# Twenty-eight pairs of unread products on TensorE ahead of the first transposes of a graph-network stack

## The chip, the core and the metric

The kernel runs on one core of a Trainium2 chip. The core's engines are TensorE (PE in the profile; its weight loads are PEld), VectorE (DVE), ScalarE (ACT), GpSimd (POOL) and SyncE (SP), which here issues the loads from HBM. The metric is the time of one execution on the device in microseconds (us), lower is better.

## The reference

A stack of four graph layers over N = 3327 nodes with D = 64 features and a dense 3327 x 3327 matrix `adj` of weights, most of them zero. Every layer normalizes, clips at zero, propagates and adds to x:

```python
# layer 0: two GRU cells, each with one propagation
def _ggc(x, adj, W, wih, whh, bih, bhh):
    m = adj @ (x @ W)
    gi = m @ wih.T + bih
    gh = x @ whh.T + bhh
    ...
    return (1.0 - z) * n + z * x
h = jnp.maximum(_layernorm(x, axis=-1), 0.0)
x = x + _L0_gnn_ref(h, adj, ...)
# layer 1: weights 0.5 ** (rank from the end of the row's neighbours), one propagation
# layer 2: w = adj * adj, three times x = w @ x; x = x @ W.T + b
# layer 3: twice x = tanh(concat([adj @ x, x]) @ W[k])
```

In all there are eight propagations, each a product of a 3327 x 3327 matrix with a 3327 x 64 one.

## The kernel before

The nodes are padded to 3328 = 26 blocks of 128. The host hands over `adj` transposed; x lies in SBUF as `xs`, 128 partitions by 13 blocks by two halves by 64 features. It is loaded in two transfers (line 119): first the blocks of chunk 0 (three blocks, 384 columns of 128 partitions), then the rest.

The 13 blocks are cut into four chunks of 3, 3, 3 and 4 blocks, in two groups (chunks 0 and 1; chunks 2 and 3). A tile of the adjacency is 128 source nodes by the columns of one group in both halves, 768 or 896 KB; SyncE loads the tiles (line 405) in the order of their use into 20 slots, each load waiting until its slot is free.

A propagation (`propagate`, line 607) takes one tile and one chunk and issues two f32 matmuls, one for each half, with 64 output partitions and 384 or 512 columns each; both halves share a PSUM bank and use the upper and lower 64 partitions. The list `units` holds all these steps in the order in which TensorE runs them. It begins with `alone(0, 0, ...)`: the first propagation for group 0, one tile after the other, chunk 0 then chunk 1. Beside it a count of nonzero entries runs (`count`, line 542, bf16 matmuls on a mask which VectorE makes at line 466).

Everything on an engine runs in the order in which the program issues it. Ahead of the list come four tasks `before_0`, one for each chunk, which the program advances in a fixed interleaving:

```python
def before_0(c):
    h = nodes(c)
    yield from layernorm_relu(h, c)
    y[0][c] = h
    yield 12.0 + 3.0 * c
    transpose_to_features(h, c)
```

`layernorm_relu` (lines 834 to 849) is VectorE work except for one power on GpSimd (line 845); it writes the features `y`. `transpose_to_features` (line 791) turns chunk c's features by six f32 matmuls with the identity on TensorE, and ScalarE copies the result out (line 793). The transposes of chunk 0 are the first instructions on TensorE, and the propagation follows.

PSUM has eight banks, four named `sum` and four named `temp`. `take()` hands out a free one, `give(i)` returns it; which one is next follows from how long ago each was returned. Nothing else schedules: bank choices and order are made when the program is built.

Of the kernel before, what the change touches and what calls it, by code (L numbers as in the profile page):

```python
# [91 lines left out]
def upper(n):  # L92
    return slice(n * D, (n + 1) * D)
# [3 lines left out]
def kernel(  # L97
# [9 lines left out]
    nc = tc.nc  # L107
# [9 lines left out]
    xs = const.tile([P, NB, 2, D], F32, name="xs")  # L117
# [39 lines left out]
    def unfold_cell(cell):  # L157

        n = 3 * D + (NBIAS if cell == 0 else 0)
        i, ps = take()  # L160
        for h in range(2):
            nc.tensor.matmul(ps[upper(h), :n], ident[:, :D], stage[:, 4 * D:4 * D + n], start=True, stop=True)
        v = ps[:, :3 * D].rearrange("p (g f) -> p g f", f=D)
        for h in range(2):
            nc.vector.tensor_copy(cells[upper(1 - h), cell, h, 0:3], v[upper(1 - h)])
        if cell == 0:
            nc.vector.tensor_copy(bcol, ps[:, 3 * D:n])
        give(i)

    def fold_cell(cell):  # L170
# [67 lines left out]
    def more_constants():  # L238
# [7 lines left out]
        load_cell(0)  # L246
        yield 20.0
        unfold_cell(0)
        yield 1.0

# [27 lines left out]
        load_cell(1)  # L278
        yield 20.0
        unfold_cell(1)  # L280
        yield from fold_cell(1)
        yield 30.0
# [13 lines left out]
    def blocks(c):  # L296
        return CH[c][1] - CH[c][0]

    def width(c):
        return blocks(c) * P  # L300
# [15 lines left out]
    def take(sums=False, either=True):  # L316


        either = either and not sums
        pool = idle_sums if sums else idle_temps  # L320
        if either and idle_sums and (not pool or released[idle_sums[0]] < released[pool[0]]):
            pool = idle_sums
        for c in list(tasks):
            if not pool and c not in running:
                advance(c)
        i = pool.popleft()
        return i, banks[i]

    def give(i):
        released[i] = max(released) + 1  # L330
        (idle_sums if i < 4 else idle_temps).append(i)
# [5 lines left out]
    def flat(t):  # L337
        return t.rearrange("p b s d -> p b (s d)")
# [4 lines left out]
    def xchunk(c):  # L343
        return xs[:, CH[c][0]:CH[c][1]]
# [8 lines left out]
    def advance(c):  # L353
        running.add(c)
        try:
            tasks[c][1] = next(tasks[c][0])
        except StopIteration:
            del tasks[c]
        running.discard(c)

    def begin(c, task):
        finish(c)
        tasks[c] = [task, 0.0]
        advance(c)
# [274 lines left out]
    def alone(g, k, sweep, lag=None, parts=False):  # L639
        tiles = [Tile(q, g, KIND[k] == SQUARED) for q in sources_of(*range(NC))]  # L640
        counting = Counting(g, lag)
        chunks = (GROUPS[g][0], *PARTS) if parts else GROUPS[g]
        for t in tiles[:NQ - sweep]:
            for c in chunks:
                put(k, c, t)
            if lag is not None:
                counting.add(t)
        for c in chunks:
            for t in tiles[NQ - sweep:]:
                put(k, c, t)  # L650
                if lag is not None and c == GROUPS[g][0]:
                    counting.add(t)
        counting.rest()
# [277 lines left out]
# [6 lines that stand above are left out]
# [96 lines left out]
    joint(1, 6, sweep=8, later=4, keep=4)  # L1033
    alone(0, 7, sweep=6, parts=True)

    for c in (0, 0, 1, 0, 1, 2, 1, 2, 3, 2, 3, 3):
        if c in tasks:
            advance(c)
        else:
            begin(c, before_0(c))  # L1040
# [45 lines left out]
```

## Time and profile before

| | |
|---|---|
| time, median of 3 runs | 706.93 us (705.94 to 707.05) |
| span of the profiled execution, first to last instruction | 703.7 us |
| other time of the profiled execution | none is given on its page |
| TensorE busy | 679.8 us, 97% of the span |
| VectorE, ScalarE, GpSimd busy | 350.1, 271.8, 80.0 us |
| first matmul | at 14.92 us |
| mean granted TensorE clock | 0.999 |
| read from HBM | 199.45 MB, 285 GB/s over the span |

The runs' times are of whole executions on the device; the profile's span runs from the first to the last instruction of one execution, and its times are counted from the span's start. A row such as `128*64 128x384 f32` is a matmul with 128 rows in, 64 out and 384 columns. `x12` is a number of records. Text in brackets is the idle time of the engine before the row and what ended it.

### The profile page before, as it was taken

How to read it: one execution, taken by the hardware profiler on the slowest of the kernel's cores; microseconds unless marked ns; L12 is line 12 of the kernel's file. 1: busy time of each engine (PE TensorE's matmuls, PEld its weight loads, DVE VectorE, ACT ScalarE, POOL GpSimd, SP SyncE). 2: the span in 40 equal slices, each digit the busy share in tenths (PEclk: the TensorE clock that was granted, in tenths of full speed). 3: DMA queues.
4: the chain of work that ended last, by engine and by line, in shares of the span. 5: the costliest groups of instructions: out<-in, count | busy, mean ns of one | idle time of the engine just before them, and what ended most of it. 6: DMA issues, size and time to landing. Idle time of an engine off the chain costs nothing.

```text
span 703.7 us, 12628 instructions
## 1 busy us (share of the span) xinstructions
PE 679.8 (97%) x5100; PEld 372.9 (53%) x5100; DVE 350.1 (50%) x746; ACT 271.8 (39%) x422; POOL 80.0 (11%) x114
## 2 busy tenths in 40 slices
PE   1999999999999999999999999999999999999997
PEld 1454666643556787677444444333344444344586
DVE  7556835643997889847523105425271565005101
ACT  1014100122146888888998206832166600000101
POOL 4300000002284233111100000000000000000000
PEclk9999999999999999999999999999999999999999
DMA  9999996089686952683799649973998399927991
GB/s 344 401 385 404 406 405 241 2 314 398 209 279 253 371 177 76 246 297 96 265 390 343 245 151 409 405 276 100 398 366 271 107 391 406 406 81 276 402 403 45
DMA packets 68549, 201.31 MB, mean 286 GB/s; under 512 B 7228, under 2 KB 8228, under 8 KB 68492
## 3 DMA queue, kind: packets, MB, share of 16 engines
q1 hardware_dynamic: 65596, 199.46, 75.9%
q8 instruction: 40, 0.66, 0.4%
q10 hardware_dynamic: 720, 0.85, 0.3%
q0 software_dynamic: 2176, 0.20, 0.2%
q14 instruction: 17, 0.14, 0.1%
HBM read 199.45 MB, written 0.85 MB: 285 GB/s over the span
## 4 chain that ended last, share of the span: by engine, by line
PE 91%; DVE 7%; issue 0%; ACT 0%; DMA 0%; POOL 0%; ACTq 0%; DVEq 0%; POOLq 0%
PE sum L607 77%; PE temp L307 5%; PE temp L542 2%; PE temp L876 2%; PE sum L307 1%; DVE adj L466 1%; PE temp L774 1%; PE sum L876 1%; DVE e L521 1%; DVE st L842 1%; DVE adj L901 1%; DVE t L836 1%; DVE y L841 0%; DVE st L834 0%; DMA xs<-in_x 0%
## 5 line engine op out<-in xcount | busy, mean ns | idle before, releaser
L607 PE MATMUL sum<-adj,y 128*64 128x384 f32 (+3 forms) x3016 | 534.5, 502 | 0.7 <-DVE y L849 0.6
L607 PEld LDWEIGHTS sum<-adj,y 128*64 128x64 f32 x3016 | 243.5, 137 | 237.3 <-issue 212.4
L440 ACT ACTIVATE adj<-adj 128x768 f32<-128x768 f32 (+1 forms) x176 | 144.2, 893 | 45.8 <-PE sum L607 21.9
L466 DVE TENSOR_SCALAR adj<-adj 128x768 bf16<-128x768 f32 (+3 forms) x208 | 114.0, 597 | 39.8 <-PE temp L542 31.8
L824 ACT COPY both<-sum 64x384 f32<-64x384 f32 (+3 forms) x17 | 8.1, 478 | 192.6 <-PE sum L607 191.4
L607 PE MATMUL sum<-e,both 128*64 128x384 bf16 (+1 forms) x624 | 78.5, 339 | 0.5 <-DVE e L521 0.5
L523 ACT ACTIVATE e<-temp,bitsb 128x384 int16<-128x384 f32 (+1 forms) x117 | 66.0, 605 | 15.1 <-PE temp L307 9.9
L825 DVE COPY both<-sum 64x384 f32<-64x384 f32 (+3 forms) x17 | 9.6, 569 | 110.5 <-ACT both L824 110.5
L307 PE MATMUL temp<-adj,tri 128*64 128x384 bf16 (+1 forms) x332 | 56.8, 341 | 0.5 <-DVE e L521 0.2
L442 DVE TENSOR_TENSOR adj<-adj 128x768 f32<-128x768 f32 (+1 forms) x32 | 30.6, 1005 | 52.1 <-DMA adj<-in_adjT 33.4
L845 POOL TENSOR_TENSOR st<-st,mhalf 128x6 f32<-128x6 f32 (+1 forms) x16 | 24.0, 1498 | 283.2 <-DVE st L843 279.5
L607 PEld LDWEIGHTS <-both 128*64 128x64 bf16 x624 | 46.6, 110 | 15.5 <-issue 2.2
L307 PEld LDWEIGHTS <-tri 128*64 128x64 bf16 x416 | 33.5, 110 | 15.3 <-issue 7.1
L521 DVE TENSOR_SCALAR e<-temp 128x384 int16<-128x384 f32 (+1 forms) x49 | 30.1, 617 | 21.1 <-ACT e L523 10.5
L471 POOL DMA_DIRECT2D adj<-totals x52 | 31.5, 607 | 51.2 <-PE temp L307 40.9
L803 DVE STREAM_TRANSPOSE both<-y 32x96 f32<-32x96 f32 (+1 forms) x128 | 35.6, 278 | 2.9
L542 PE MATMUL temp<-adj,behind 128*64 128x384 bf16 x208 | 30.3, 339 | 0.9 <-DVE adj L466 0.7
L819 DVE STREAM_TRANSPOSE y<-t 32x96 f32<-32x96 f32 (+1 forms) x64 | 17.8, 278 | 24.9 <-ACT t L810 24.0
L542 PEld LDWEIGHTS <-behind 128*64 128x64 bf16 x208 | 17.0, 110 | 17.6 <-issue 15.9
L755 DVE COPY t<-sum 128x384 f32<-128x384 f32 x6 | 3.3, 555 | 35.3 <-PE sum L607 35.3
L564 POOL MEMSET adj<- 128x768 f32 (+1 forms) x2 | 1.9, 950 | 145.3 <-PE sum L607 145.3
L523 ACT ACTIVATE e<-sum,bitsb 128x384 int16<-128x384 f32 (+1 forms) x28 | 16.6, 598 | 2.5 <-PE sum L307 2.1
(132 smaller groups left out, 327.8 us busy)
## 6 DMA issues: line engine op xcount, KB each, us to landing
adj<-in_adjT SPq DMA_DIRECT2D x130, 768.0 KB, 8.5
adj<-in_adjT SPq DMA_DIRECT2D x104, 896.0 KB, 12.3
xs<-in_x SPq DMA_DIRECT2D x1, 640.0 KB
adj<-totals POOLq DMA_DIRECT2D x26, 3.0 KB, 5.1
adj<-totals POOLq DMA_DIRECT2D x26, 3.5 KB, 3.0
out<-xs ACTq DMA_DIRECT2D x2, 192.0 KB
out<-xs ACTq DMA_DIRECT2D x1, 256.0 KB
stage<-in_weights SPq DMA_DIRECT2D x2, 112.0 KB, 13.1
```

Source lines behind the costliest of these rows:

```text
L307: nc.tensor.matmul(out[hs], lhsT[:, hs], rhs, start=start, stop=stop)
L440: nc.scalar.activation(sq, v, AF.Square)
L442: nc.vector.tensor_tensor(sq, v, v, ALU.mult)
L466: nc.vector.tensor_scalar(t.mask.view[:rows, half], t.view()[:rows, half], 0.0, None, op0=ALU.not_equal)
L471: nc.gpsimd.dma_start(out=t.mask.view[P - 1:P], in_=totals[t.g][t.q:t.q + D + 1:D, :])
L521: nc.vector.tensor_scalar(wide[:, s], ps[:, :w], BITS, 0.0, op0=ALU.add, op1=ALU.max)
L523: nc.scalar.activation(wide[:, s], ps[:, :w], AF.Relu, bias=bitsb)
L542: nc.tensor.matmul(counts[c][1][s * D:(s + 1) * D, :w], behind[:, NQ - 1 - t.q:NQ - 1 - t.q + D], t.mask.view[:, s, t.cols(c)], start=firs ...
L607: nc.tensor.matmul(acc[h][1][h * D:(h + 1) * D, :w], yq[h], rhs[h], start=first and n == 0, stop=last and n == len(terms) - 1)
L803: nc.vector.transpose(to[at:at + 32, :, q], h[q * 32:(q + 1) * 32, :, s, f * 32:(f + 1) * 32])
L845: nc.gpsimd.tensor_tensor(st[:, 3, :n], st[:, 2, :n], mhalf[:, :n], ALU.pow)
L876: nc.tensor.matmul(ps[upper(1 - s), :w], cells[:, cell, s, g, :], both[c][:, s], start=True, stop=True)
```

## The change

A function `warm_up` is added and called once, ahead of the four `before_0` tasks. It takes a PSUM bank, issues 28 pairs of f32 matmuls whose both operands are rows of x from the first transfer (64 columns of x as weights, the 384 columns of chunk 0 as the moving operand; one product into the upper, one into the lower 64 partitions of the bank), and gives the bank back. Nothing reads what they write.

```diff
+    def warm_up():
+
+        i, ps = take()
+        for n in range(28):
+            for h in range(2):
+                nc.tensor.matmul(ps[upper(h), :width(0)], xs[:, 0, h, :], flat(xchunk(0)), start=True, stop=True)
+        give(i)
...
+    warm_up()
     for c in (0, 0, 1, 0, 1, 2, 1, 2, 3, 2, 3, 3):
         if c in tasks:
             advance(c)
```

On TensorE the 56 products stand ahead of the transposes of chunk 0. In the profile of the changed kernel, lines behind the new function have numbers higher by 8.

## The prediction

> **What bounds the kernel now.** I read the busy times first, then TensorE's waits, then the timeline of the first 26 us, and last the weight loads one by one.
>
> Part 1 of the page and the shares by engine of the chain that ended last say who sets the end:
>
> ```profile
> PE 679.8 (97%) x5100; PEld 372.9 (53%) x5100; DVE 350.1 (50%) x746; ACT 271.8 (39%) x422; POOL 80.0 (11%) x114
> PE 91%; DVE 7%; issue 0%; ACT 0%; DMA 0%; POOL 0%; ACTq 0%; DVEq 0%; POOLq 0%
> ```
>
> TensorE (PE) is busy for 679.8 of 703.7 us, and the chain runs through it for 91%. What it does not fill is in the view of waits for TensorE alone (us in total, times, longest):
>
> ```profile
> PE temp L791 <- DVE y L849: 14.9, 1, 14.9
> PE sum L307 <- DVE e L521: 1.4, 2, 0.9
> PE temp L542 <- DVE adj L466: 0.7, 2, 0.5
> PE sum L607 <- DVE y L849: 0.6, 1, 0.6
> PE sum L607 <- DVE e L521: 0.5, 1, 0.5
> ...
> PE sum L607 <- DVE both L825: 0.2, 1, 0.2
> ```
>
> One wait of 14.9 us at the start, for the normalized features of the first chunk; after it all waits together are 4.1 us, every one for VectorE. No row has TensorE waiting for a transfer. So from 14.92 us on, the kernel is one nearly unbroken stream of matmuls, and whatever moves its start or its rate in the first microseconds moves the end. The timeline shows that start (start, duration, engine, line):
>
> ```profile
> 3.22 0.55 DVE L834 TENSOR_REDUCE st<-xs 128x6 f32<-128x384 f32 x1 [3.22 <-DMA xs<-in_x]
> ...
> 14.31 1.49 DVE L849 SCALAR_TENSOR_TENSOR y<-t,st 128x384 f32<-128x384 f32 x3
> ...
> 14.92 1.55 PE L791 MATMUL temp<-ident,y 128*64 128x128 f32 x12 [14.92 <-DVE y L849]
> 16.26 9.41 PE L607 MATMUL sum<-adj,y 128*64 128x384 f32 x48
> 25.50 0.49 PE L542 MATMUL temp<-adj,behind 128*64 128x384 bf16 x4
> ```
>
> The first rows of x are there at 3.22 us. Between that and 14.92 VectorE and GpSimd run the layer norm, and TensorE has 11.7 us of nothing. The weight loads of the first propagation matmuls give the rate of TensorE:
>
> ```profile
> 17.54 0.24 PEld L607 LDWEIGHTS sum<-adj,y 128*64 128x64 f32 x2 [0.40 <-issue]
> 18.18 0.24 PEld L607 LDWEIGHTS sum<-adj,y 128*64 128x64 f32 x2 [0.40 <-issue]
> 18.82 0.24 PEld L607 LDWEIGHTS sum<-adj,y 128*64 128x64 f32 x2 [0.40 <-issue]
> 19.37 0.14 PEld L607 LDWEIGHTS sum<-adj,y 128*64 128x64 f32 x2 [0.32 <-issue]
> 19.69 0.14 PEld L607 LDWEIGHTS sum<-adj,y 128*64 128x64 f32 x2 [0.18 <-issue]
> 20.02 0.14 PEld L607 LDWEIGHTS sum<-adj,y 128*64 128x64 f32 x2 [0.18 <-issue]
> ```
>
> Each line stands for two matmul records. Lines start 0.64 us apart up to 18.82, and 0.3225 apart from 19.37 on: TensorE begins at half speed. The line between them took 0.55 us; with s the moment of the change, (s - 18.82)/0.64 + (19.37 - s)/0.3225 = 1 gives s = 19.28. So the first 4.36 us of work (14.92 to 19.28) run at half rate and lose 2.18 us against full rate. The granted clock of the profile does not show this:
>
> ```profile
> 14.92:19.27 4.35, 4.35 (x22) 2.52 (x24) 3.76 (x6) 0.94 (x2) 4.26 (x6) 1.00 1.03 401
> ```
>
> This is the view by stretches; the 1.00 behind the busy times is the granted clock, in the very stretch where the spacing is double. I therefore go by the spacing and not by that column.
>
> **The change, part by part.**
>
> *What one pair costs.* The added call issues 28 times two products, 56 matmuls with 128 rows in, 64 out and 384 columns in f32: the shape of the f32 propagation matmuls of line 607, in both halves of the output as there. In the trace an f32 matmul leaves two records: the first transposes are 6 in the program and x12 in the trace; the first six tiles at line 607 are 24 matmuls and x48. So a pair is four records, two of the lines above: 0.645 us at full rate, 1.28 at half. Test: from 16.26 to 25.50 lie 12 pairs; 3.02 us at 1.28 give 2.4, and 6.22 us at 0.645 give 9.6, 12.0 in all. The two halves do not come cheaper than this; whatever overlap there is between them is already in the 0.645.
>
> *How long the 28 take.* 28 x 0.645 = 18.06 us at full rate. They begin cold, so they take over the half-rate stretch, 2.18 us more: 20.24 us.
>
> *Where they lie.* The first product waits for the first load of x alone, which released VectorE at 3.22. 3.22 + 20.24 = 23.46 us. TensorE's queue is in order: behind the last product stand the transposes of chunk 0 (line 791 of before), and behind these the whole propagation. The gap in which the products are free ends at 14.92; it has room for (11.70 - 2.18)/0.645 = 14.8 pairs. The other 13.2 pairs are on the path.
>
> *What comes back.* The transposes and first tiles find the clock already up: the 2.18 us which they lost is gone, since TensorE is not idle for a moment between the last product and the first transpose (y is ready at 14.9, and the first tiles have long landed). So the stream starts 23.46 - 14.92 = 8.54 us later and is 2.18 us shorter: +6.36 us. The length of the half-rate stretch cancels if it is the same as before; in short, 3.22 + 18.06 - 14.92.
>
> *Is the delay absorbed?* Only where TensorE now waits for something that does not move with it. Of the 4.1 us of later waits the two for masks (0.7) stand near 79 us, where VectorE works through its own queue of results that TensorE made; they move too. I take 0 and keep 0.7 as the bound. The loads get further ahead, but no wait for a load is there to shrink; in this part the queue of loads itself waits for slots that TensorE and VectorE free. VectorE, ScalarE and GpSimd wait longer at the start, for no price: the chain enters TensorE at 14.92 and stays in it but for the 7% of VectorE, most of which is the layer norm ahead of it.
>
> *Banks.* The products hold one PSUM bank and give it back, so the rotation of the banks moves by one and several results (transposes, gates) change between the two groups of four banks. Apart from that, the order on every engine is the same; only the 56 products are new. No row shows what another rotation costs. It could add or remove waits of TensorE for the engine that empties a bank; all such waits after 14.92 are 4.1 us and the longest is 0.9. I take 0, bounds -0.7 and +0.7.
>
> *The clock's spread.* The trace has one half-rate stretch, so its variation isn't seen directly. The three runs, each with one, lie within 1.1 us (705.94 to 707.05), so I let the loss differ by 1.1 us either way.
>
> *A rule against it.* The Trainium skill, page "TensorE: Matmul & The Clock Gate", section "Part 1: The HAM clock gate", says that the clock is at half rate by default and opens after a full busy window of about 3.4 us which runs freely, a budget of time and not a number of matmuls. The 4.36 us of the trace agrees with that. By the rule alone the stretch would be 3.4 to 6.8 us, and the change, as an estimate from that page, +5.9 to +7.6 us; and it would say that anything issued past that window in front of ready work is pure cost.
>
> **Sum.** Span 703.7 + 6.4 = 710.0. The page gives no time of the profiled execution beyond its span; the median of the runs, 706.93, is 3.2 above it, for what lies around the span, and the change does not touch that. 706.93 + 6.36 = 713.3 us, slower by 0.9%. Bounds: 6.36 - 1.1 - 0.7 = +4.6 (711.5) to 6.36 + 1.1 + 0.7 = +8.2 (715.1).
>
> **Rivals.**
>
> *The products fit in the gap: faster.* If a pair cost one line of the above (0.32 us, both halves at once) instead of two, 28 pairs would end at 3.22 + 2.18 + 9.03 = 14.43, before 14.92, and only the warm clock would be left: -2.18, 704.8 us. The decision point is a price of 0.34 us a pair for hiding all, and 0.418 for breaking even (3.22 + 28p = 14.92). For it: the gap is real, and so is the half rate. Against it: 12 pairs in 9.24 us, in the same shape. 4%.
>
> *The start has slack.* If the loads paced the first 100 us (the DMA engines are at 9 tenths there), a later start would be caught up, and neither delay nor clock would count: 706.9. Against it: no wait for a load on TensorE. 2%, with the chance that the products are not run at all since nobody reads them; the built program does hold them. Between this and the forecast, a partial catching up, +1.4 to +4.6: 4%.
>
> *The clock does not open for these products, or opens late.* All 28 at 1.28 us are 35.8 us, ending at 39.1; with a warm stream behind them this is 39.1 - 14.92 - 2.18 = +22.0, 728.9 us; with a cold start behind them, 731.1. For it: the trace has no product of this operand, and nothing on TensorE so early. Against it: same shape, same density as what opened the clock at 19.28. 3%.
>
> **How the numbers follow.** Forecast 87%, 713.3, own range 711.5 to 715.1. The rest is 13%, so the range need not reach further. No change that can be told means within 0.2%, 1.4 us. Faster 0.04, same 0.02, slower 0.94 (0.87 + 0.04 + 0.03).
>
> **What would show it.** In the profile of the changed kernel: the first matmul at about 3.2 us; 112 records of the new line; weight loads 0.64 apart for some 4.4 us, then 0.32; the first transposes at 23.5 without a wait on TensorE for VectorE, taking 0.8 us (as the later ones of chunk 1 do) rather than 1.55; 12 pairs of first tiles in 7.7 us rather than 9.24; later waits near 4 us in sum; span near 710. Transposes at 14.9 would make the first rival right; a start at 23.5 with a span under 706 the second; spacing of 0.64 beyond 10 us the third.

## The result, and the profile after

The changed kernel takes 712.35 us (median of 4 runs, 711.64 to 713.30) against 706.43 us (4 runs, 705.80 to 707.05): 5.9 us more, ratio 1.0087 with a 95% interval of 1.0073 to 1.0101. The forecast was 713.3 us, range 711.5 to 715.1.

The profiled execution of the changed kernel took 712.66 us, and its span was 710.7, 7.0 above the 703.7 shown before. The span before was a low one: the 26 runs of that kernel beside the first experiments have spans from 702.9 to 705.5, their middle at 704.5. That explains most of why the two profiles differ by 7.0 us and the medians by 5.9.

Part 1 of the page and the shares of the chain by engine:

```profile
PE 698.1 (98%) x5212; PEld 379.8 (53%) x5212; DVE 349.6 (49%) x746; ACT 271.9 (38%) x422; POOL 80.7 (11%) x114
PE 87%; issue 5%; DVE 4%; DMA 1%; POOL 1%; ACT 0%; ACTq 0%; POOLq 0%; DVEq 0%
```

TensorE has 112 records more and 18.3 us more of work; the other engines have what they had. (Lines of the program are 8 higher than before: 799 is the old 791, 615 the old 607, 550 the old 542.) The start of TensorE in the timeline:

```profile
3.32 20.44 PE L175 MATMUL temp<-xs 128*64 128x384 f32 x112 [3.32 <-DMA xs<-in_x]
23.59 0.82 PE L799 MATMUL temp<-ident,y 128*64 128x128 f32 x12
24.25 7.91 PE L615 MATMUL sum<-adj,y 128*64 128x384 f32 x48
31.99 0.49 PE L550 MATMUL temp<-adj,behind 128*64 128x384 bf16 x4
```

The products start with the landing of x and hold the queue until 23.59, 8.67 us past the old start of the transposes. VectorE had finished the first chunk's features at the old time: in this profile too its final step (old line 849) starts at 14.40, so during the last 8.7 us of the products TensorE has real work ready and standing in the queue. The transposes take 0.82 us instead of 1.55, the first six tiles 7.74 us (24.25 to 31.99) instead of 9.24. At the first count the stream is 31.99 - 25.50 = 6.49 us late. The weight loads show where the half-rate stretch went:

```profile
6.58 0.24 PEld L175 LDWEIGHTS temp<-xs 128*64 128x64 f32 x2 [0.40 <-issue]
7.22 0.24 PEld L175 LDWEIGHTS temp<-xs 128*64 128x64 f32 x2 [0.40 <-issue]
7.79 0.14 PEld L175 LDWEIGHTS temp<-xs 128*64 128x64 f32 x2 [0.34 <-issue]
8.12 0.14 PEld L175 LDWEIGHTS temp<-xs 128*64 128x64 f32 x2 [0.18 <-issue]
```

0.64 us apart up to 7.22, 0.32 from 7.79 on; the same working as before puts the change at 7.72, 4.40 us after the first product. From the first count to about 228 us the distance to the old profile stays at 6.5. The last 0.5 us of the 7.0 arises between 266 and 347 us, where the view of waits has a row that the old one lacks, TensorE waiting 0.4 us for a small transfer that GpSimd issues:

```profile
PE temp L315 <- DMA adj<-totals: 0.4, 1, 0.4
```

### The profile page after: what moved, and what is told of

Same layout as the page of the kernel before. It is cut to its first block, busy times and chain, and to the rows that moved or that the text cites. A ratio compares the mean times of both kernels' runs of the same rounds, so it can differ in the third digit from the quotient of the medians.

```text
span 710.7 us, 12852 instructions
## 1 busy us (share of the span) xinstructions
PE 698.1 (98%) x5212; PEld 379.8 (53%) x5212; DVE 349.6 (49%) x746; ACT 271.9 (38%) x422; POOL 80.7 (11%) x114
## 4 chain that ended last, share of the span: by engine, by line
PE 87%; issue 5%; DVE 4%; DMA 1%; POOL 1%; ACT 0%; ACTq 0%; POOLq 0%; DVEq 0%
PE sum L615 72%; PE temp L315 4%; PE temp L175 3%; PE temp L550 2%; PE temp L884 2%; PE sum L315 1%; PE sum L884 1%; PE temp L782 1%; POOL adj L479 1%; DMA adj<-totals 1%; DVE adj L474 1%; DVE adj L909 1%; DVE e L529 0%; DMA xs<-in_x 0%; POOL st L853 0%
## 5 line engine op out<-in xcount | busy, mean ns | idle before, releaser
L479 POOL DMA_DIRECT2D adj<-totals x52 | 37.6, 725 | 51.8 <-PE temp L315 42.2
L529 DVE TENSOR_SCALAR e<-temp 128x384 int16<-128x384 f32 (+1 forms) x49 | 30.1, 618 | 21.7 <-ACT e L531 10.5
L175 PE MATMUL temp<-xs 128*64 128x384 f32 x112 | 20.4, 531 | 3.3 <-DMA xs<-in_x 3.3
L572 POOL MEMSET adj<- 128x768 f32 (+1 forms) x2 | 1.6, 802 | 151.7 <-PE sum L615 151.7
```

The costliest lines, as they stand in the source:

```text
L175: nc.tensor.matmul(ps[upper(h), :width(0)], xs[:, 0, h, :], flat(xchunk(0)), start=True, stop=True)
L479: nc.gpsimd.dma_start(out=t.mask.view[P - 1:P], in_=totals[t.g][t.q:t.q + D + 1:D, :])
L529: nc.vector.tensor_scalar(wide[:, s], ps[:, :w], BITS, 0.0, op0=ALU.add, op1=ALU.max)
```

## The experiments

The theory: a pair costs 0.645 us, the half-rate stretch adds about 2.2, and everything is free until the features are ready at 14.9; past that, each pair delays the whole stream, and in return the stream loses its own half-rate stretch. The rivals differ from run to run. All edits are against the changed kernel unless said otherwise.

**14 pairs.**

```diff
-        for n in range(28):
+        for n in range(14):
```

> 14 pairs in place of 28. Theory (a pair costs 0.645 us, the half-rate stretch of 4.4 us adds 2.2, free until the features are ready at 14.9): 3.3 + 9.0 + 2.2 = 14.5, so the products end 0.4 us before the transposes could start. Start unchanged, the 2.2 us at half rate gone from the stream: 2.2 us under the kernel before, ratio about 0.997. Rival (the clock is not what the products change, and any work ahead of the transposes costs something): at or above the kernel before.

Measured: 704.15 us against 706.45 (26 runs), ratio 0.9968 (0.9956 to 0.9981). 2.3 us under the kernel before, as the theory has it; its timeline:

```profile
3.23 10.65 PE L175 MATMUL temp<-xs 128*64 128x384 f32 x56 [3.23 <-DMA xs<-in_x]
14.90 0.88 PE L799 MATMUL temp<-ident,y 128*64 128x128 f32 x12 [1.02 <-DVE y L857]
15.61 7.91 PE L615 MATMUL sum<-adj,y 128*64 128x384 f32 x48
```

The transposes again start when VectorE releases them, and run at full rate. The gap of 1.0 us did not close the clock. The first count is 2.15 us earlier than before. Not all of that reaches the end in this profile. TensorE waits for a tile:

```profile
55.77 1.51 PE L615 MATMUL sum<-adj,y 128*64 128x384 f32 x8 [0.63 <-DMA adj<-in_adjT]
```

The same matmuls start at 57.12 in the kernel before, and the count just ahead of them at 56.80 against 54.65: the lead falls from 2.15 to 1.35 us. The span is 1.3 us shorter than the one before (702.4 against 703.7, the low one). That the medians differ by 2.3, so near to 2.2, is in part luck.

**18 and 42 pairs.** Same line, 18 and 42.

> 18 pairs. Theory: 3.3 + 11.6 + 2.2 = 17.1, transposes 2.2 us late, stream 2.2 us shorter: even with the kernel before within 0.3 us. Rival (delay is partly caught up later): 0.5 to 2 us under the kernel before.

> 42 pairs. Theory (every pair past the 14.8th is on the path): 14 x 0.645 = 9.0 us above the kernel with 28 pairs, 15 us above the kernel before. Rival (part of a delay is absorbed, more so the later the start, as the loads run ahead): 5 us or less above the kernel with 28 pairs.

Measured: 706.72 us against 706.44, ratio 1.0003 (0.9994 to 1.0012): even. And 721.71 us, ratio 1.0213 (1.0199 to 1.0227), 9.4 us above the kernel with 28. From 18 to 42 pairs the time grows by 15.0 us, 0.625 us a pair, against 0.645 from the weight loads. Some runs with 18 pairs have up to 2.8 us outside their span, where the other kernels have about 2; by the medians of the spans (704.3 and 719.75) it is 0.644 a pair. Nothing of a delay is absorbed that these runs can tell, up to 42 pairs: in the profile with 42 the stream is 16.0 us late at line 162 (61.4 against 45.4) and still 16.0 at old line 774 (167.7 against 151.7).

**One half only.** 28 single products into the upper 64 partitions.

```diff
-            for h in range(2):
+            for h in range(1):
```

> 28 single products into the upper 64 partitions only, none into the lower. Theory (the two halves of a pair overlap on TensorE, so that one costs as much as both): 0.645 us each, 3.3 + 18.1 + 2.2 = 23.6, as slow as 28 pairs, 6 us above the kernel before. Rival (one after the other, half a pair each): 0.32 us each, end at 14.5, 2.2 us under the kernel before.

Measured: 712.34 us, ratio 1.0081 (1.0067 to 1.0095), as slow as 28 pairs. Its weight loads come one record at a time, at the spacing which had two before:

```profile
9.20 0.14 PEld L175 LDWEIGHTS temp<-xs 128*64 128x64 f32 x1 [0.19 <-issue]
9.52 0.14 PEld L175 LDWEIGHTS temp<-xs 128*64 128x64 f32 x1 [0.18 <-issue]
```

So the two halves of a pair do overlap; the second product of each is free. The price of 0.645 is that of the overlapped pair. The end of the products shows something more:

```profile
22.74 0.43 PE L799 MATMUL temp<-ident,y 128*64 128x128 f32 x2
23.06 0.81 PE L175 MATMUL temp<-xs 128*64 128x384 f32 x2
23.39 0.43 PE L799 MATMUL temp<-ident,y 128*64 128x128 f32 x2
```

Four records of the transposes start ahead of the last product record (23.71), which stands before them in the program. So the order on TensorE, which the description of the kernel and the prediction take as strict, is, by the starts that the profile gives, not kept to the last microsecond here; with pairs no row shows this.

**Half the columns.**

```diff
-                nc.tensor.matmul(ps[upper(h), :width(0)], xs[:, 0, h, :], flat(xchunk(0)), start=True, stop=True)
+                nc.tensor.matmul(ps[upper(h), :192], xs[:, 0, h, :], groups(xchunk(0))[:, 0:3], start=True, stop=True)
```

> 28 pairs with 192 columns in place of 384. Theory (the price goes by columns): 0.32 us a pair, 3.3 + 9.0 + 2.2 = 14.5, hidden, 2.2 us under the kernel before. Rival (a fixed price of each record stands beside the columns, 0.1 us and more of four records): a pair at 0.45 us or more, end at 18.1 or later, 1 us or more above the kernel before.

Measured: 704.66 us, ratio 0.9975 (0.9966 to 0.9984). The products run from 3.27 to 14.16 us and are hidden: 10.9 us for 28 pairs at half the width. The price goes by columns.

**4 pairs, early.** Same line, 4.

> 4 pairs in place of 28, at the same place: 3.3 + 2.2 + 2.6 = 8.1, then TensorE idles 6.8 us until 14.9. Theory (the clock falls back to half rate over such a gap): first transposes 1.5 us long, first tiles at 1.28 a pair again, time as the kernel before. Rival (once opened, the clock stays open over 6.8 us): transposes 0.8 us long, 2.2 us under the kernel before.

Measured: 706.88 us, ratio 1.0007 (0.9999 to 1.0016): nothing is gained. The timeline has the transposes at 1.55 us again:

```profile
3.13 4.52 PE L175 MATMUL temp<-xs 128*64 128x384 f32 x16 [3.13 <-DMA xs<-in_x]
14.80 1.55 PE L799 MATMUL temp<-ident,y 128*64 128x128 f32 x12 [7.15 <-DVE y L857]
16.14 9.97 PE L615 MATMUL sum<-adj,y 128*64 128x384 f32 x48
```

Here the granted clock shows the fall. In the view by stretches, the number ahead of the last two (DMA share, GB/s) is the clock:

```profile
9.00:10.00 1.00, 0.00 (x0) 0.00 (x0) 0.93 (x3) 0.00 (x0) 0.89 (x1) 1.00 1.05 427
10.00:10.50 0.50, 0.00 (x0) 0.00 (x0) 0.47 (x2) 0.00 (x0) 0.00 (x0) 0.55 1.01 406
10.50:11.00 0.50, 0.00 (x0) 0.00 (x0) 0.47 (x2) 0.00 (x0) 0.00 (x0) 0.50 1.01 399
```

A mean of 0.55 between 10.0 and 10.5 puts the fall to half at 10.05, 2.4 us after the last product ended (7.65).

**4 pairs, late.** The call is moved from the head into the layer norm of chunk 2, and multiplies its centred rows, which VectorE writes just before 9.8 us.

```diff
-        for n in range(28):
+        for n in range(4):
             for h in range(2):
-                nc.tensor.matmul(ps[upper(h), :width(0)], xs[:, 0, h, :], flat(xchunk(0)), start=True, stop=True)
+                nc.tensor.matmul(ps[upper(h), :width(0)], t[:, h, :], t[:, :6], start=True, stop=True)
...
-    warm_up()
...
         nc.vector.tensor_tensor(xc[:, :n], v, st[:, 1, :n, None].to_broadcast([P, n, D]), ALU.subtract)
+        if first:
+            warm_up(xc)
...
-        yield from layernorm_relu(h, c)
+        yield from layernorm_relu(h, c, first=c == 2)
```

> 4 pairs again, but on the centred rows of chunk 2, which VectorE writes at about 9.9 us, so that they lie just ahead of the transposes: 9.9 + 2.2 + 2.6 = 14.7. Theory (what counts is some 4.4 us of work that reaches up to the transposes): 2.2 us under the kernel before, like 14 pairs. Rival (a longer stretch of work is needed, or the products are too few): the first transposes at half rate still, time between the kernel before and 1 us under it.

Measured: 704.41 us, ratio 0.9972 (0.9963 to 0.9982). Four pairs do what 14 do if they reach up to the transposes; with four in both, the place decides. In this profile they were just enough, though:

```profile
9.81 5.11 PE L175 MATMUL temp<-t 128*64 128x384 f32 x16 [9.81 <-DVE t L844]
```

The transposes follow at 14.82 and take 0.88. The products' weight loads stay 0.64 us apart up to the last at 13.70, so nearly all of the four pairs ran at half rate (5.11 us, about 2.6 at full rate). Fewer pairs at this place were not tried.

**Bank rotation alone.** `warm_up` takes and gives a bank and multiplies nothing.

> No products; a PSUM bank is taken and given back, so the rotation of the banks is that of the changed kernel. Theory (the rotation is worth nothing): within 0.3 us of the kernel before, first transposes at 14.9 us at half rate. Rival (the rotation adds the new wait for the rows that GpSimd's queue brings, 0.4 us in the profile after): 0.5 us above the kernel before, with that wait.

Measured: 706.28 us, ratio 0.9995 (0.9986 to 1.0004). The rotation costs nothing that these runs can tell, and the wait for GpSimd's transfer is not in its profile. That wait is not in the profile with 42 pairs either, which has the same rotation. So the rotation alone does not bring it; what does is open.

**An earlier start, without products.** Against the kernel before: the interleaving of the layer norms alone.

```diff
-    for c in (0, 0, 1, 0, 1, 2, 1, 2, 3, 2, 3, 3):
+    for c in (0, 0, 0, 1, 0, 1, 1, 2, 1, 2, 2, 3, 2, 3, 3, 3):
```

> No products; the kernel before with another interleaving of the four chunks' layer norms, so that chunk 0's features are finished at about 7.9 us and its propagation starts there, its transposes later. Theory (the start of TensorE's stream sets the end one for one): 14.9 - 8.0 = 6.9 us under the kernel before. Rival (the loads pace an early start: a 768 KB tile takes 1.96 us at 401 GB/s and TensorE needs one each 1.29 to 1.61 us): waits for loads appear on TensorE, and the gain is 3 to 5 us.

Measured: 703.76 us against 706.53, ratio 0.9968 (0.9956 to 0.9981): 2.8 us, neither the theory's 6.9 nor quite the rival's 3 to 5, and the rival's mechanism. TensorE starts at 8.08 and meets the loads, then the masks that VectorE makes:

```profile
8.08 7.18 PE L607 MATMUL sum<-adj,y 128*64 128x384 f32 x32 [8.08 <-DVE y L849]
15.71 1.51 PE L607 MATMUL sum<-adj,y 128*64 128x384 f32 x8 [0.45 <-DMA adj<-in_adjT]
17.66 1.51 PE L607 MATMUL sum<-adj,y 128*64 128x384 f32 x8 [0.44 <-DMA adj<-in_adjT]
19.92 0.32 PE L542 MATMUL temp<-adj,behind 128*64 128x384 bf16 x1 [0.75 <-DVE adj L466]
```

Starts are 1.95 us apart there: the rate at which the tiles land. Between 18 and 62 us its weight loads wait another 3.7 us for tiles (ten pauses, the ordinary 0.18 us of each included). The lead over the kernel before shrinks from 3.5 us at line 162 (41.9 against 45.4) to 2.0 at line 774 (74.4 against 76.4), where it stays. With 14 pairs, too, TensorE catches up with the loads, once, at 55.77 us, for 0.6 us; in the profile before there was no such wait.

**The earlier start and 3 pairs.** Both edits.

> The same, with 3 pairs of products on x ahead of it: 3.3 + 3 x 1.28 = 7.2, just before the features are ready. Theory (start and clock add up): up to 2.2 us under the kernel without products. Rival (where loads pace the first tiles, a faster clock only waits for the next tile): even with the kernel without products, with longer waits for loads.

Measured: 704.52 us, ratio 0.9968 (0.9956 to 0.9979): even with the earlier start alone, the rival. Starts of the first tiles are 1.9 to 2.0 us apart from the first on, now with five waits for loads of 0.35 to 0.46 us up to 18.2. The two gains do not add. By the leads above, the waits for tiles and masks take back what is above some 2 us. Every version that wins (14 pairs, 4 late ones, the narrow ones, the earlier start, both together) beats the kernel before by about the same 0.3%.

## Why the prediction was right

*What bounds the kernel.* TensorE's stream from its first useful matmul on. The later start went through to the end unshortened: +6.49 us at 32 us, +6.5 at 228 us; and 18, 28 and 42 pairs lie within 0.6 us of a line of slope 0.625 us. One reading behind this was wrong: of the 7% that the chain spends on VectorE, 46.7 us, only 11 are the layer norm ahead of the stream. The rest stands later; from 66.83 to 79.34, for instance, the chain is on VectorE although TensorE waits no more than 0.7 us there. That a delay passes through those stretches is shown by the runs, not by that sentence.

*The price of a pair.* 0.645 us predicted. The products of the changed kernel took 20.27 us from first start to the transposes, 28 x 0.645 + 2.20. The reading that was most open to doubt, whether the 0.645 already holds the overlap of the halves, is settled by the single products: one costs what two cost.

*Free room.* 14.8 pairs predicted; 14 fit with 1.0 us to spare, 18 break even. The break-even of the first rival, 3.22 + 28p = 14.92, read for pairs instead of price, is 18.1.

*The half-rate stretch.* That it moves to the products and leaves the stream was right; that it is the same size each time was not. That it came out equal in the two profiles, so that the stream was 6.49 us late at the first count where 6.36 had been worked out, is luck. It measured 4.36 us before, 4.40 after, and from the weight loads of other runs 2.8 (18 pairs), 2.9 (14), 5.2 (one half), 5.3 (bank alone) and 5.3 (42), so that half of it, the loss, lies between 1.4 and 2.7 us. The bound of 1.1 us which I took from the spread of three runs does not quite cover the difference of two such losses, up to 1.3 us between single executions, and it came from a bad argument: the runs differ for other reasons too. The kernel with 4 late pairs, with no half-rate work on its path in its profile, still spreads over 1.8 us.

*The base.* I gave 3.2 us as the time around the span. It is about 2.0 (712.66 beside a span of 710.7); the other 1.2 was the profiled execution being faster than the median. The forecast was made as a difference, so this did not enter it.

*No absorption.* Right for a delay. I had read "no wait for a load on TensorE" as meaning that the loads have no say at all; the experiments toward the other side show that they are just behind, about 2 us of earlier start away.

*The rivals.* The first (hidden, faster) has the mechanism of the 14 pairs and of the narrow ones, with its 2.2 us measured as 1.8 to 2.3; for 28 full pairs its price was wrong by two, as argued. The second fell with 42 pairs. The third needed products that don't open the clock, and it opened at 7.72. The Trainium skill's rule on the clock, weighed in the prediction, told the right thing against the change: a few microseconds of work in the right place do (4 late pairs, 704.41 us), and the rest is cost. The stretches seen here run from 2.8 to 5.5 us. The Trainium skill's page "TensorE: Matmul & The Clock Gate", section "Part 1: The HAM clock gate", gives a busy window of about 3.4 us; the 2.8 and 2.9 us measured with 18 and 14 pairs are shorter than the least that the prediction read out of it, 3.4.

The 0.4 us between forecast (+6.4) and measurement (+5.9, interval 5.2 to 7.1) is not resolved; it is within what the half-rate stretch varies.

## What to carry to other kernels

Work that nobody reads can bring TensorE to full rate ahead of its first real matmul, but it stands before that matmul in the same queue: size it in microseconds to end just before the data are ready, counting the first stretch at double price, and put it late rather than make it long. Price a matmul by its spacing in the trace, for the shape and with the neighbour that overlaps it, not by its number of instructions. Before moving a start forward, look how far behind the loads are.

## What the runs showed of the hardware that was not expected

The granted clock in the profile reads 1.00 in the first half-rate stretch of every kernel here, and 0.50 in the second one of the kernel with 4 early pairs:

```profile
14.80:20.30 5.50, 5.50 (x26) 3.00 (x28) 4.89 (x7) 0.94 (x2) 5.35 (x7) 0.50 1.03 402
```

The column knows of a fall but not of the state at the start. The clock fell 2.4 us after the last product, and after that fall it took 5.5 us of work to come back (14.80 to 20.30), against 3.5 us the first time in the same execution. An f32 product into 64 partitions costs the same alone as with a second one into the other 64 beside it.
